# Macaron block on Trainium2: transposes one group later, a first head in two parts, paired updates, an early bias

## The chip, the cores and the metric

The kernel runs on one core of one Trainium2 chip. Five engines work side by side, each through its own list of instructions: PE (matrix products), DVE and POOL (elementwise work), ACT (activations and copies) and SP (here it only issues transfers, or DMAs). The metric is the time of one execution on the device in microseconds (us). Three runs of the kernel before took 3453.76, 3454.74 and 3462.36 us; their median, 3454.74, is the time to compare with.

## The reference

One transformer block on x of shape 4 x 1024 x 512 in float32: half a feed-forward layer, attention, and half the same feed-forward layer again.

```python
x = x + 0.5 * ffn(layernorm(x))
x = x + attention(layernorm(x))
x = x + 0.5 * ffn(layernorm(x))

def ffn(x):                      # 512 -> 2 x 2048 -> 512
    gate, up = split(x @ quant(w_gate_up).T)
    return rms_norm(silu(gate) * up) @ quant(w_proj).T

def attention(x):                # 32 query heads, 8 key heads, 16 wide
    Q, K = rope(x @ Wq.T + bq), rope(x @ Wk.T + bk)
    V = x @ Wv.T + bv
    w = softmax(Q @ K.T / 4)     # 1024 x 1024 for each head
    return (w @ V) @ Wo.T + bo
```

`quant` rounds each group of 64 weights to -1, 0 or 1 times the group's mean magnitude, in bf16.

## The kernel before

**Tiles and blocks.** x stays on the chip in tiles of 128 rows (`xt[b, i]`, eight for each batch). The feed-forward layer works on blocks of 512 rows (four tiles), so there are eight blocks for the first half layer and eight for the second. It splits the 2048 hidden columns into 16 chunks. To keep precision, an operand is split into a rounded part and a remainder (`xT` and `xL`, `high` and `low`), and both are multiplied.

**The order of work is written by hand.** Inside `tc.manual_schedule()` each engine executes its instructions in the order in which the code issues them, and waits at an instruction until its inputs and the buffer it writes are free. The DMAs that a queue issues (SP's by `nc.sync`, POOL's by `nc.gpsimd`) stand in the same order as that engine's other work. So moving a call in the code moves its instructions on every engine at once.

**The stages.** They follow each other:

- The first stage (to about 217 us in the profile) quantises and transposes the weights, and runs the first half layer of blocks 0 and 1 beside it. `First.group(i)` (L639 to L683) is one round: it finishes earlier chunks, turns the three weight parts of chunk i (`transpose`, L490), starts the products of chunk i (`start`), and lets DVE quantise the next weights (`signs`, `quantize`, `scales`). In rounds 0 and 1 it also normalises two of the four tiles of block 1 each and transposes them: `normalize` yields for each tile a function that transposes it on PE, copies it on ACT (`xT`) and subtracts on DVE (`xL`); these are called `turn`. The rest of block 1's projections follows in `projection`, to about 265 us.
- An input stage for each batch (`input_output`, L810 to L847) makes Q, K and V. Its loop goes over eight tiles, with work of several tiles in flight: `turn_in` transposes tile n, `project` multiplies tile n-1, `rotate` (DVE and POOL) and `turn` (PE transposes `pqT`, then writes of `d_q` and `d_k` to memory by SP) finish tile n-2. At n from 5 to 8 it prepares the four tiles of the next feed-forward block. In batches 1 to 3 it also runs the output product of the batch before: `put(i)` multiplies tile i of the attention's result `aT` with the output weights into `pa`, adds the bias on DVE (`ao`) and adds that to x on POOL. `put` 0 to 5 stand in the loop, 6 and 7 after it. `aT` is a load from memory, multiplied on POOL by the reciprocals `rec` of the softmax's sums (`divide`, L996 to L1016, in three steps: `invert`, `spread`, `multiply`).
- A feed-forward stage (`FeedForward.chunks`, L310 to L345). Products with the projection follow their hidden chunk two chunks behind. When the last chunk of a block is projected, `factors` computes the norm and `end` updates the four tiles of x on DVE, and SP stores them if the block is finished. Beside it runs the first part of the maxima, below (`early`).
- An attention stage (`Attention.run`, L1143 to L1238) of 128 steps: eight groups of four query heads that share a key head, two halves of queries, eight tiles of keys. A step computes scores `s`, exponentials `e` on ACT, and the product `o` with V, one step later. The softmax's row maxima come from a second pass over the scores: `maxima` (L1050) computes `sm` on PE, and DVE reduces it. For each group the maxima are turned to `mrow`, written to memory (`d_m`, a DMA on POOL's queue), read back as `mT`, and subtracted by a third product in the scores. Most steps hold two maxima; some hold four, where the number left demands it: `READY` is the step by which the last ought to be complete.
- After the last attention an output stage without an input (`output`, L792 to L808), then the last feed-forward stage.

**Loads for the heads.** `Places` keeps buffers of three tiles and loads them in a fixed order as they come free. `load_heads` (L728) loads the queries and the keys of a group as three DMAs on SP: `p_m<-d_q`, and `p_m<-d_k` twice, for the maxima; `p_s` has the same for the scores. With `places.slow` set, a load's DMAs are queued as pieces, and `piece` issues one.

```python
READY = (HKV - 1) * STEPS - 4                    # 108
places.done(("in", new.b))                       # after the loop
places.load(("m", new.b, 0))
```

Of the kernel before, what the change touches and what calls it, by code (L numbers as in the profile page):

```python
# [10 lines left out]
F32 = mybir.dt.float32  # L11
# [3 lines left out]
ALU = mybir.AluOpType  # L15
# [4 lines left out]
P = 128  # L20
D = 512
H = 2048
HQ, HKV, HD = 32, 8, 16
# [8 lines left out]
DC = D // P  # L32
# [4 lines left out]
def tile_macaron_block(  # L37
# [17 lines left out]
    nc = tc.nc  # L55
    B, T, _ = x.shape
    NT = T // P
# [28 lines left out]
    xt = {}  # L86
# [54 lines left out]
    class FeedForward:  # L141
# [135 lines left out]
            nc.vector.tensor_scalar(half, inv, 0.5, None, ALU.mult)  # L277
            return half

        def end(self, k, half):  # L280
            b, tb, which = self.blocks[k]
            new = waiting.pop(0) if which == "z" and waiting else None
            if new is not None:
                slots[new] = slots[b, tb]
            for i, t in enumerate(self.tiles(k)):
                nc.vector.scalar_tensor_tensor(  # L286
                    t, self.pos[k][i], half[:, i : i + 1], t, ALU.mult, ALU.add
                )
# [20 lines left out]

        def chunks(self):  # L310
            last = len(self.order) - 1
            due = []
            for n, (k, hc) in enumerate(self.order):
                if self.beside is not None:
                    places.piece()
                parts, rest = self.hidden(k, hc)
                due.append((k, hc, parts))
                behind = due.pop(0) if len(due) > self.LAG else None
                if behind is not None:
                    self.project(*behind, [0, 1])  # L320
                if n == last:
                    rest()
                if self.beside is not None:
                    self.beside(self.ps, (n - self.begin) / (last - 1 - self.begin))
                if behind is not None:
                    self.project(*behind, [2, 3])
                    if behind[1] == HC - 1:
                        self.end(behind[0], self.factors(behind[0]))
                if n < last:
                    rest()  # L330
                if k + 1 < len(self.blocks) and 4 <= hc < 12 and hc % 2 == 0:
                    for turn in self.normalize(k + 1, [hc // 2 - 2], self.wp, self.ps, "gu"):
                        self.later.append((hc + 1, turn))
                for step in [step for step in self.later if step[0] == hc]:
                    self.later.remove(step)
                    step[1]()

            for i in range(4):
                for behind in due:
                    self.project(*behind, [i])  # L340
                if i == 1:
                    half = self.factors(k)
            self.end(k, half)
            for _, step in self.later:
                step()  # L345

    class First(FeedForward):
# [7 lines left out]
        def groups(self):  # L355

            self.kept = tc.tile_pool(name="kept", bufs=1)
            self.banks = tc.tile_pool(name="fp0a", bufs=4, space=PSUM)
            self.keep, self.ps = self.kept.__enter__(), self.banks.__enter__()
            self.w, self.wb, self.wide, self.twice, self.q = {}, {}, {}, {}, {}  # L360
            self.sg, self.made, self.units, self.parts, self.turns = {}, {}, {}, {}, []
# [277 lines left out]
        def group(self, i):  # L639
# [13 lines left out]
            if i < 2:  # L653
                if i > 0:
                    self.start(0, i)
                some = [2 * i, 2 * i + 1]
                self.signs(i + 1)
                self.quantize(i + 1)
                steps = self.scales(i + 2)
                scales = normal_scales(self.tiles(1, some), f"0a_1_{i}")  # L660
                for turn in self.normalize(1, some, self.wp, self.ps, "gu", 4, scales):
                    turn()
            else:
                steps = self.scales(i + 2)
                self.start(1, i - 2)
                self.signs(i + 1)
# [60 lines left out]
    def load_heads(key, tiles):  # L727

        _, b, g = key
        q, k = at[b].d_q, at[b].d_k  # L730
        sources = [q[g * G * HD : (g + 1) * G * HD].rearrange("m r t -> (m r) t")]
        for part in range(2):
            keys = k[part, g * HD : (g + 1) * HD].rearrange("d r t -> (d r) t")
            sources.append(keys.unsqueeze(0).to_broadcast([G, 2 * HD, T]))
        return [
            lambda t=t, src=src: nc.sync.dma_start(t.bitcast(F32), src)
            for t, src in zip(tiles, sources)
        ]

# [68 lines left out]
        turns[3]()  # L808

    def input_output(new, old, put, then, wp, ps):  # L810
        turn = None
        for n in range(NT + 2):
            if n == 0:
                new.normalize(0, wp, new.scales(0))
            if 1 <= n <= NT:
                new.project(n - 1, ps)
            if n >= 2:
                new.rotate(n - 2)
            scales = new.scales(n + 1) if n + 1 < NT else None
            after = normal_scales(then.tiles(0, [n - 5]), f"f_{new.b}_{n}") if 5 <= n < 9 else None  # L820
            if n >= 2:
                new.rotated_sum(n - 2)
            if scales is not None:
                new.normalize(n + 1, wp, scales)
            behind, turn = turn, None
            if after is not None:
                (turn,) = then.normalize(0, [n - 5], wp, ps, "pt", 2, after)
            if behind is not None:
                behind()
            if put is not None:  # L830
                for i in {4: (0,), 5: (1,), 6: (2,), 7: (3,), 8: (4,), 9: (5,)}.get(n, ()):
                    put(i, range(DC))
            if n < NT:
                new.turn_in(n, wp, ps)
            if n >= 2:
                new.turn(n - 2, wp, ps)
            if put is not None and n == 1:
                old.after.pop(0)()
                old.after.pop(0)()
            if put is not None and n == 2:  # L840
                old.after.pop(0)()

        places.done(("in", new.b))
        places.load(("m", new.b, 0))
        if put is not None:
            for i in (6, 7):
                put(i, range(DC))  # L847

    class Attention:

# [15 lines left out]
        STEPS = NB * NT  # L866
        ITEMS = NT * 2
        TOTAL = HKV * ITEMS * G
        READY = (HKV - 1) * STEPS - 4
        FIRST = 3  # L870
        EARLY = (3 * ITEMS - 1) * G

# [43 lines left out]
                    [xt[self.b, i]], f"a_{self.b}_{i}", wp, "xa", 2, scales  # L916
                )

        def turn_in(self, i, wp, ps):
            label = f"a_{self.b}_{i}"  # L920
            self.xTs[i] = wp.tile([P, DC, P], F32, tag="axT", name=f"axT_{label}", bufs=2)
            turned(self.rows.pop(i), label, ps, "pt", self.xTs[i])

        def project(self, i, ps):
            pq = ps.tile([P, D], F32, tag="pq", name=f"pq_{self.b}_{i}", bufs=2)
# [65 lines left out]
        def divide(self, c, wp):  # L991
# [12 lines left out]
            def invert():  # L1004
                nc.vector.reciprocal(narrow, narrow)
                nc.sync.dma_start(d_r.rearrange("h (a t) -> h a t", t=n), narrow)
                nc.sync.dma_start(a, self.d_o[at, 0])

            def spread():
                nc.sync.dma_start(rec, d_r.unsqueeze(1).to_broadcast([8, HD, T]))  # L1010
# [7 lines left out]
        def project_out(self, wp, ps, bufs):  # L1018
# [4 lines left out]
            pas = {}  # L1023

            def put(i, chunks):
                if i == 0 and DC - 1 in chunks:
                    nc.sync.dma_start(b_o, bo.partition_broadcast(P))
                if 0 in chunks:
                    pas[i] = ps.tile([P, D], F32, tag="pa", name=f"pa_{b}_{i}", bufs=bufs)
                for n, w in enumerate(w_out):  # L1030
                    for c in chunks:
# [319 lines left out]
```

## Time and profile before

| what | value |
|---|---|
| median of three runs | 3454.74 us |
| the profiled execution | 3450.52 us |
| its span | 3448.8 us |
| mean granted PE clock | 0.977 |
| PE busy | 3317.4 us, 96% |
| DVE busy | 2172.1 us, 63% |
| ACT busy | 1763.7 us, 51% |
| POOL busy | 936.0 us, 27% |

The profile is of one execution. An engine is busy while one of its instructions runs; the time in which it waits is put down to the instruction that it waited for, by the name of what that one wrote. PE is busy in nearly all of the span, and its idle time is spread over a hundred short waits. The granted clock tells how much of its full rate PE had: the same instruction takes longer at a lower one. A row such as `PE sm L1061 <- DMA p_m<-d_k` reads: PE's instruction that writes `sm` at line 1061 waited for the DMA that writes `p_m` from `d_k`.

The stages in the profile, from the starts of their instructions: input stages at about 265 to 331 us, 990 to 1075, 1735 to 1820 and 2478 to 2560; attention at about 650 to 990, 1403 to 1735, 2147 to 2478 and 2892 to 3216; the output stage from 3216 to 3262; feed-forward between them and to the end.

### The profile page before, as it was taken

How to read it: one execution, taken by the hardware profiler on the slowest of the kernel's cores; microseconds unless marked ns; L12 is line 12 of the kernel's file. 1: busy time of each engine (PE TensorE's matmuls, PEld its weight loads, DVE VectorE, ACT ScalarE, POOL GpSimd, SP SyncE). 2: the span in 40 equal slices, each digit the busy share in tenths (PEclk: the TensorE clock that was granted, in tenths of full speed). 3: DMA queues.
4: the chain of work that ended last, by engine and by line, in shares of the span. 5: the costliest groups of instructions: out<-in, count | busy, mean ns of one | idle time of the engine just before them, and what ended most of it. 6: DMA issues, size and time to landing. Idle time of an engine off the chain costs nothing.

```text
span 3448.8 us, 57082 instructions
## 1 busy us (share of the span) xinstructions
PE 3317.4 (96%) x22744; PEld 2150.2 (62%) x22744; DVE 2172.1 (63%) x3626; ACT 1763.7 (51%) x2346; POOL 936.0 (27%) x907
## 2 busy tenths in 40 slices
PE   4998999999999999999999999999999999999899
PEld 3777777644467777544477777444577776444587
DVE  6976666677635666777355666777256656775243
ACT  4752333577742333688723333788523334788343
POOL 2663433200123343100033333000143332010244
PEclk7999999999999999999999999999999999999999
DMA  3533222122313223133123221222231221232111
GB/s 99 155 115 91 69 76 77 44 89 94 101 59 97 69 72 101 51 104 102 65 76 90 82 76 55 73 93 91 82 108 54 81 89 56 94 98 71 30 46 56
DMA packets 206507, 278.47 MB, mean 81 GB/s; under 512 B 25248, under 2 KB 151200, under 8 KB 206240
## 3 DMA queue, kind: packets, MB, share of 16 engines
q1 hardware_dynamic: 201120, 272.70, 25.6%
q8 instruction: 179, 2.93, 0.4%
q0 software_dynamic: 5120, 2.11, 0.3%
q14 instruction: 88, 0.72, 0.1%
HBM read 216.01 MB, written 58.72 MB: 80 GB/s over the span
## 4 chain that ended last, share of the span: by engine, by line
PE 84%; DVE 6%; DMA 3%; issue 3%; POOL 2%; ACT 1%; SPq 0%; POOLq 0%; DVEq 0%; ACTq 0%
PE gu L211 22%; PE s L1158 18%; PE o L1179 14%; PE po L251 12%; PE sm L1061 7%; PE pq L929 3%; PE pa L1032 2%; PE gu_0a L533 2%; DMA p_m<-d_k 1%; DVE pm L1070 1%; PE pkv L929 1%; DVE x L286 1%; DMA rec<-d_r 1%; PE pxn L136 1%; PE po_0a L251 1%
## 5 line engine op out<-in xcount | busy, mean ns | idle before, releaser
L1070 DVE TENSOR_REDUCE pm<-sm 128x1 f32<-128x512 f32 x2048 | 1284.6, 684 | 385.3 <-PE sm L1061 381.7
L1169 ACT ACTIVATE e<-s 128x1024 f32<-128x1024 f32 x1024 | 996.4, 1022 | 326.3 <-PE s L1158 323.5
L1061 PE MATMUL sm<-p_m,p_m 32*128 32x512 f32 x4096 | 768.7, 440 | 31.4 <-DMA p_m<-d_k 10.3
L211 PE MATMUL gu<-xT,guT 128*128 128x512 f32 x1792 | 707.3, 395 | 0.7 <-ACT xT L137 0.7
L211 PE MATMUL gu<-xL,guT 128*128 128x512 f32 x1792 | 701.7, 392 | 0.3 <-DVE xL L139 0.3
L1158 PE MATMUL s<-p_s,p_s 32*128 32x512 f32 x4096 | 679.0, 441 | 0.2 <-ACT e L1169 0.2
L1158 PEld LDWEIGHTS s<-p_s,p_s 32*128 32x128 f32 x4096 | 315.5, 186 | 457.6 <-ACT e L1169 435.2
L1179 PE MATMUL o<-e,vs 128*32 128x512 f32 x4096 | 557.4, 617 | 1.8 <-ACT e L1169 1.8
L1061 PEld LDWEIGHTS sm<-p_m,p_m 32*128 32x128 f32 x4096 | 356.1, 184 | 125.5 <-DVE h L223 65.7
L1158 PE MATMUL s<-mT,ones_r 2*128 2x512 f32 x2048 | 414.3, 399 | 7.1 <-DMA mT<-d_m 6.9
L231 POOL TENSOR_TENSOR sq<-h 128x512 f32<-128x512 f32 x210 | 218.4, 1040 | 710.2 <-DVE h L223 707.7
L221 ACT ACTIVATE sg<-gu 128x512 f32<-128x512 f32 x224 | 133.8, 597 | 497.2 <-PE gu L211 497.1
L211 PEld LDWEIGHTS gu<-xT,guT 128*128 128x128 f32 x1792 | 339.1, 189 | 75.1 <-ACT xT L137 1.0
L223 DVE TENSOR_TENSOR h<-sg,gu 128x512 f32<-128x512 f32 x224 | 153.8, 687 | 367.1 <-PE gu L211 365.8
L211 PEld LDWEIGHTS gu<-xL,guT 128*128 128x128 f32 x1792 | 338.8, 189 | 70.1 <-DVE xL L139 0.6
L251 PE MATMUL po<-w_pT,high 128*128 128x512 f32 x896 | 373.0, 416 | 0.0
L251 PE MATMUL po<-w_pT,low 128*128 128x512 f32 x896 | 353.0, 394 | 0.1
L237 ACT CAST high<-h 128x512 fp32r<-128x512 f32 x224 | 139.0, 620 | 341.9 <-DVE h L223 337.7
L100 ACT CAST guT<-g 128x512 fp32r<-128x512 bf16 x448 | 274.7, 613 | 12.3 <-ACT guT L100 5.8
L235 POOL TENSOR_TENSOR acc<-acc,sq 128x512 f32<-128x512 f32 x205 | 275.5, 1344 | 16.1
L251 PEld LDWEIGHTS po<-w_pT,high 128*128 128x128 f32 x896 | 169.1, 189 | 97.8 <-issue 66.4
L1099 POOL DMA_DIRECT2D d_m<-mrow x32 | 18.9, 591 | 757.2 <-DVE mrow L1097 757.2
(145 smaller groups left out, 3226.2 us busy)
## 6 DMA issues: line engine op xcount, KB each, us to landing
g<-d_guT SPq DMA_DIRECT2D x448, 128.0 KB
p_m<-d_k SPq DMA_DIRECT2D x64, 512.0 KB
p_s<-d_k SPq DMA_DIRECT2D x64, 512.0 KB
p_m<-d_q SPq DMA_DIRECT2D x32, 512.0 KB
p_s<-d_q SPq DMA_DIRECT2D x32, 512.0 KB
d_o<-oT SPq DMA_DIRECT2D x64, 256.0 KB
x<-in_L_attn_x_dram SPq DMA_DIRECT2D x32, 256.0 KB
w<-in_L_ffn_w_gate_up_dram SPq DMA_DIRECT2D x32, 256.0 KB
```

What stands on the lines that cost most here:

```text
L100: nc.scalar.copy(w, t)
L211: nc.tensor.matmul(pg, lhsT=self.weights[k, hc][part][:, c, :], rhs=xp[:, c, :], start=(c == 0 and low == 0), stop=(c == DC - 1 and low == 1),
L223: nc.vector.tensor_tensor(h, sg, gu[1], ALU.mult)
L231: nc.gpsimd.tensor_tensor(sq, h, h, ALU.mult)
L235: nc.gpsimd.tensor_tensor(acc, acc, sq, ALU.add)
L237: nc.scalar.copy(high, h)
L251: nc.tensor.matmul(self.pos[k][i], lhsT=h[:, i * P : (i + 1) * P], rhs=w_pT[hc], start=(hc == 0 and n == 0), stop=(hc == HC - 1 and n == 1),)
L1061: nc.tensor.matmul(s, lhsT=q[at, i * P : (i + 1) * P], rhs=k[part][at, half * 512 : (half + 1) * 512], start=(part == 0), stop=(part == 1),)
L1070: nc.vector.tensor_reduce(pm[:, i, j, half : half + 1], s, AX.X, ALU.max)
L1158: nc.tensor.matmul(s[:, e, :], lhsT=k[part][at, keys] if part < 2 else ones_r[at, :], rhs=(q if part < 2 else self.mrows[g])[at, queries], ...
L1169: nc.scalar.activation(w, s, AF.Exp, scale=1.0 / HD**0.5)
L1179: nc.tensor.matmul(o[j * SLOT : (j + 1) * SLOT, :], lhsT=vs[:, kc, g, :], rhs=es[j // 2][:, j % 2, :], start=(kc == 0), stop=(kc == NT - 1),)
```

## The change

It has six parts.

- In rounds 0 and 1 of the first stage the transposes of block 1 are kept in `turning`, and called one round later, behind the products of that round.
- In batch 0's input stage the transposes have two PSUM banks in place of one (`banks`).
- The first group's load is six DMAs in place of three: 896 columns, then 128. It begins in the loop's last round (n = 9), ahead of `turn(7)`; the rest follows after the loop. `put(6)` moves into that round too. Since `load_heads` is also used for `p_s`, the first scores are loaded in six DMAs as well.
- `end` updates tiles 0 and 1 of x at once, and 2 and 3 after the next chunk's `hidden`.
- The output bias `b_o` is loaded on POOL's queue and added to x on POOL as `put` begins; when the product is there, DVE adds it to x at once. The load of `aT` also moves from SP's queue to POOL's.
- `READY` is one step less.

```diff
-        def end(self, k, half):
+        def end(self, k, half, some=range(4)):
             b, tb, which = self.blocks[k]
-            new = waiting.pop(0) if which == "z" and waiting else None
-            if new is not None:
-                slots[new] = slots[b, tb]
-            for i, t in enumerate(self.tiles(k)):
+            if 0 in some:
+                new = self.new = waiting.pop(0) if which == "z" and waiting else None
+                if new is not None:
+                    slots[new] = slots[b, tb]
+            new = self.new
+            for i, t in zip(some, self.tiles(k, some)):
...
                 parts, rest = self.hidden(k, hc)
+                if ends:
+                    self.end(*ends.pop(), [2, 3])
...
                     if behind[1] == HC - 1:
-                        self.end(behind[0], self.factors(behind[0]))
+                        half = self.factors(behind[0])
+                        self.end(behind[0], half, [0, 1])
+                        ends.append((behind[0], half))
...
-                for turn in self.normalize(1, some, self.wp, self.ps, "gu", 4, scales):
+                rows = list(self.normalize(1, some, self.wp, self.ps, "gu", 4, scales))
+                for turn in self.turning:
                     turn()
+                self.turning = rows
             else:
+                for turn in self.turning:
+                    turn()
+                self.turning = []
                 steps = self.scales(i + 2)
                 self.start(1, i - 2)
...
+        parts = [slice(0, T)] if g > 0 else [slice(0, T - P), slice(T - P, T)]
         return [
-            lambda t=t, src=src: nc.sync.dma_start(t.bitcast(F32), src)
+            lambda t=t, src=src, at=at: nc.sync.dma_start(t.bitcast(F32)[:, at], src[..., at])
+            for at in parts
             for t, src in zip(tiles, sources)
         ]
...
-        turn = None
+        turn, banks = None, 2 if put is None else 1
...
+            if n > NT:
+
+                places.slow = True
+                places.done(("in", new.b))
+                places.load(("m", new.b, 0))
+                for _ in range(3):
+                    places.piece()
...
-                (turn,) = then.normalize(0, [n - 5], wp, ps, "pt", 2, after)
+                (turn,) = then.normalize(0, [n - 5], wp, ps, "pt", 2, after, banks)
...
-                for i in {4: (0,), 5: (1,), 6: (2,), 7: (3,), 8: (4,), 9: (5,)}.get(n, ()):
+                for i in {4: (0,), 5: (1,), 6: (2,), 7: (3,), 8: (4,), 9: (5, 6)}.get(n, ()):
                     put(i, range(DC))
...
-        places.done(("in", new.b))
-        places.load(("m", new.b, 0))
+        places.rest()
+        places.slow = False
         if put is not None:
-            for i in (6, 7):
-                put(i, range(DC))
+            put(7, range(DC))
...
-        READY = (HKV - 1) * STEPS - 4
+        READY = (HKV - 1) * STEPS - 5
...
-                nc.sync.dma_start(a, self.d_o[at, 0])
+                nc.gpsimd.dma_start(a, self.d_o[at, 0])
...
-                if i == 0 and DC - 1 in chunks:
-                    nc.sync.dma_start(b_o, bo.partition_broadcast(P))
+                if i == 0 and 0 in chunks:
+                    nc.gpsimd.dma_start(b_o, bo.partition_broadcast(P))
                 if 0 in chunks:
+                    nc.gpsimd.tensor_tensor(xt[b, i], xt[b, i], b_o, ALU.add)
...
-                    ao = wp.tile([P, D], F32, tag="ao", name=f"ao_{b}_{i}")
-                    nc.vector.tensor_tensor(ao, pas[i], b_o, ALU.add)
-                    nc.gpsimd.tensor_tensor(xt[b, i], xt[b, i], ao, ALU.add)
+                    nc.vector.tensor_tensor(xt[b, i], pas[i], xt[b, i], ALU.add)
```

More of the change, by code (lines that the diff above doesn't have):

```diff
@@ L311, in chunks @@
             last = len(self.order) - 1
-            due = []
+            due, ends = [], []
             for n, (k, hc) in enumerate(self.order):
@@ L360, in groups @@
             self.w, self.wb, self.wide, self.twice, self.q = {}, {}, {}, {}, {}
-            self.sg, self.made, self.units, self.parts, self.turns = {}, {}, {}, {}, []
+            self.sg, self.made, self.units, self.parts = {}, {}, {}, {}
+            self.turns, self.turning = [], []
             for n in range(4):
@@ L830, in input_output @@
             if put is not None:
-                for i in {4: (0,), 5: (1,), 6: (2,), 7: (3,), 8: (4,), 9: (5,)}.get(n, ()):
+                for i in {4: (0,), 5: (1,), 6: (2,), 7: (3,), 8: (4,), 9: (5, 6)}.get(n, ()):
                     put(i, range(DC))
             if n < NT:
-                new.turn_in(n, wp, ps)
+                new.turn_in(n, wp, ps, banks)
             if n >= 2:
@@ L917, in normalize, with turn_in @@
                 )
-        def turn_in(self, i, wp, ps):
+        def turn_in(self, i, wp, ps, banks):
             label = f"a_{self.b}_{i}"
             self.xTs[i] = wp.tile([P, DC, P], F32, tag="axT", name=f"axT_{label}", bufs=2)
-            turned(self.rows.pop(i), label, ps, "pt", self.xTs[i])
+            turned(self.rows.pop(i), label, ps, "pt", self.xTs[i], bufs=banks)
         def project(self, i, ps):
```

## The prediction

> **What bounds the kernel now.** I read the page first: the span is 3448.8 us (the profiled execution 3450.52), PE is busy for 3317.4 of it, 96%, and holds 84% of the chain that ended last. A change that removes no PE work can therefore give back at most the 131 us in which PE stands, and what its matmuls lose at a lower granted clock. So the second view is the list of what PE waited for:
>
> ```profile
> engine line waited for: us in total, times, longest us
> PE pxn_0a L136 <- DVE xn_0a L125: 34.5, 5, 14.9
> PE pqT L976 <- DVE p_t L967: 12.7, 7, 4.3
> PE sm L1061 <- DMA p_m<-d_k: 10.3, 3, 3.8
> PE sm L1061 <- DVE h L223: 9.6, 9, 1.2
> PE gu_0a L533 <- ACT guT L498: 9.2, 4, 3.8
> ...
> PE s L1158 <- DMA mT<-d_m: 6.9, 3, 3.0
> ...
> PE pa L1032 <- POOL aT L1013: 5.2, 1, 5.2
> PE pxn L136 <- DVE xn L125: 5.0, 2, 4.8
> ```
>
> Each row is a place that the change touches; 83 us stand here. A row counts in full only if nothing else is late at that place just after, so each place was read in its own timeline, beginning with the first stage, where PE's rows show start, duration, shape and the wait ahead:
>
> ```profile
> 42.91 1.11 PE L136 MATMUL pxn_0a<-ident,xn_0a 128*128 128x128 f32 x4 [14.87 <-DVE xn_0a L125]
> ...
> 52.85 0.79 PE L533 MATMUL gu_0a<-xT_0a,guT 128*128 128x512 f32 x1 [3.81 <-ACT guT L498]
> ...
> 64.79 1.09 PE L136 MATMUL pxn_0a<-ident,xn_0a 128*128 128x128 f32 x4 [5.96 <-DVE xn_0a L125]
> ...
> 72.27 0.47 PE L533 MATMUL gu_0a<-xT_0a,guT 128*128 128x512 f32 x1
> ```
>
> Last, busy times in stretches: the ends of the four attention stages (last 32 to 34 of 128 steps each), then the first 64 steps of batches 0 and 1; the columns are length, busy time of five engines, and PE's granted clock:
>
> ```profile
> core 0: us, PE busy (x) PEld busy (x) DVE busy (x) ACT busy (x) POOL busy (x), PEclk, DMA share, GB/s
> 905.10:989.80 84.70, 82.05 (x680) 34.12 (x679) 25.15 (x49) 61.20 (x65) 6.60 (x9) 0.92 0.21 65
> 1649.40:1735.20 85.80, 82.31 (x706) 34.14 (x705) 27.04 (x52) 63.68 (x68) 6.59 (x9) 0.96 0.19 64
> 2393.90:2477.70 83.80, 81.57 (x706) 35.16 (x705) 27.05 (x52) 63.45 (x68) 6.61 (x9) 0.96 0.20 65
> 3139.20:3216.30 77.10, 76.34 (x681) 32.82 (x678) 21.48 (x38) 61.17 (x65) 4.93 (x6) 1.00 0.13 44
> 655.20:825.50 170.30, 165.73 (x1697) 73.28 (x1689) 132.96 (x219) 128.42 (x136) 10.13 (x16) 0.99 0.23 75
> 1403.50:1564.60 161.10, 160.00 (x1622) 73.95 (x1620) 123.17 (x204) 124.27 (x132) 10.10 (x16) 0.97 0.25 80
> ```
>
> The fourth end has the same work as the others, no wait for mT in it and a clock of 1.00: it is 6.7 to 8.7 us shorter.
>
> **1. Transposes of the second block, one group later.** PE now waits 14.87 us for the first normalised row of block 1 before it may take the products of weight chunk 1, whose weights were quantised at 37.8. With the transposes behind those products, PE turns the three weight parts next. What was late: the DVE ran two subtractions xL (44.68, 47.71) ahead of h (48.32), and ACT two copies ahead of the cast that guT (52.21) follows. Behind them, h falls to about 43.9, guT to 44.5, and the products start at about 45.1 instead of 52.85. In the second group the row of 64.79 waits for DVE, which quantises to 59.6 and takes scales to 61.4; DVE's next signs start at 73.69 now, after a copy of 72.19 that PE's products release, and at about 65.0 when nothing there waits for the transposes. The gain is what reaches that DVE step, 73.69-65.0 = 8.7; at least the 3.81 that falls away before 52.85 whatever comes later, at most every wait of PE between 37.8, where those weights are ready, and 52.85: 5.1 (42.91-37.8), 1.95, 0.55 and 3.81, or 11.4. I take 8.7, the row that DVE's order sets. Cover: DVE's own quantising; without it the 34.5 comes back elsewhere.
>
> **2. Two banks for the transposes of the first input stage.** There PE waits 1.91, 1.40 and 0.86 for xL at L139, as pxn and pxn_a share a bank, and 4.33 for p_t at 330.07. The p_t chain is started by the last projection, which begins 1.91+1.40 = 3.3 earlier with two banks; the last wait stays. Gain 3.3, bounds 0 and 4.3.
>
> **3. First head in two parts; two output products ahead of the last turn.** In batches 1 to 3 the last pqT waits 1.80, 1.80 and 1.79 for p_t, then two products pa of 3.5 each follow. One of them moves ahead of the turn, longer than the wait: gain 5.4. The DMAs p_m<-d_q and p_m<-d_k were issued at 1073.2 to 1074.9 (batch 1), behind the writes of the last tile, landed 17.04 later, and sm waited 3.66, 2.79 and 3.83 (10.3); the matmuls after it are slow (sm 0.69 against 0.44) and lose, summed over the stretch to the next full-speed row, 1.3, 0 and 2: 3.3 more. Now seven eighths of the columns are issued at about 1067.5, ahead of tile 7's writes, and need seven tiles only; they land near 1083.5, PE wants them at about 1085.5. The last 128 columns follow the writes and land near 1088.5; the second group of maxima needs them at about 1092. Three more issues on SP cost 0.4 to 0.6 each, and wait for part one's landing; behind them on SP is only the fetch of weights three chunks ahead. Gain 13.6; bounds 3 (part one as late as now less the 3 us that its issue moves) and 13.6.
>
> **4. Two DMAs and the add of the bias to POOL.** aT<-d_o goes from SP's queue to POOL's, free of some 3 us of SP issues ahead of it; rec<-d_r behind it on SP goes earlier. In batches 1 and 2 POOL's multiply (2.35) waited 4.68 for rec at 1005.29, ahead of the rotation, and PE stood 0.73 and 2.04: gain 2.8. Against it, b_o's load is now issued on POOL at the first output product and x+=b_o (1.27) waits for it, with the rotation of the next tile queued behind: the load lands 4 to 6 us after issue (d_m's small load: 1.8 to 8.0, median 4.2), the rotation follows some 5 to 6 later. I charge 1, from 0 to 6 (2 per batch).
> The Trainium skill, page "DMA: Bandwidth & Descriptors", section "Issuing engines are not separate DMA queues", says that DMAs of all engines end on the same 16 DMA engines, and that another issuer saves only the issue time. By it the 2.8 would be 0 to 1 and the sum 2 us less; the trace has the aT load waiting on SP's order, not on bandwidth (DMA 0.2 busy), so I keep 2.8.
>
> **5. Updates of x in pairs.** At eight block ends in the four long feed-forward stages, sm waits 0.84 to 1.25 for h (9.2 in all), because DVE runs four updates x (2.73 together) ahead of h. With two updates ahead, h comes 1.37 earlier, more than any wait; the last two follow h and only delay the next po, whose first product is one chunk away (about 11 us). Gain 9.1, bounds 4 and 9.6. The four waits for x (3.3) are at stage ends and stay.
>
> **6. The last output stage.** Now each x of a tile passes ao on DVE (0.69), then POOL (1.26), one buffer between: 2.07 per tile. With b_o added ahead, DVE alone needs 0.69 plus statistics. x0 to x3 are ready at about 3243.9 instead of 3247.5, statistics end at 3247.1, the first transposes run at 3249.2 (now 3253.18, after a wait of 4.76), and the first product at about 3255.9 instead of 3262.46, since products pa no longer stand between: gain 6.5. The multiply that PE awaits for 5.16 is now behind b_o's landing and six adds (6 x 1.27 = 7.6) on POOL, and so is the issue of the last aT load: about 3228 instead of 3223.4. The loads of aT and rec ended together at 3234.8, 11.4 after the first issue; rec now goes first and alone, so the pair ends between 1 earlier and 3 later; I charge 1. Net 5.5, bounds 0 and 8.
>
> **7. Maxima complete one step earlier.** mT arrives one step (2.47) earlier; the waits were 1.97, 3.04, 1.86. Gone with them is the slow stretch: from step 96 to the end the stages take 83.60, 84.69, 82.73 against 75.97: 7.6+8.7+6.8 = 23.1; batch 1 keeps a rest of 0.6. The price: three more steps with four maxima per batch. The first 64 steps of batch 0 hold 16 such, those of batches 1 to 3 hold 4: (170.3-161.6)/12 = 0.72 each, by 12 is 8.7. Net 13.8 (13.5 taken); bounds -9 (waits stay) and 14.
> A rule speaks against the larger term: the page "TensorE: Matmul & The Clock Gate", section "The two states you'll see", gives about 3.4 us of idleness before the clock falls. By it waits of 2 to 3 us cost only themselves, 6.9-8.7 = -1.8, and the whole sum would be 15 less. The rows differ: o's eight matmuls take 1.94 after the 1.97 wait and 1.07 before it.
>
> **Sum.** 8.7 + 3.3 + (5.4+13.6) + (2.8-1) + 9.1 + 5.5 + 13.5 = 60.9. On the profiled execution 3450.5-60.9 = 3389.6; the median of the runs is 4.2 above it: about 3394.
>
> **Rivals.** (a) mT stays late, since d_m's write and its reading back share DMA engines with tables and loads (d_m to mT 3.7 to 8.2 us): term 7 becomes -8.7, the time 3416. For it: batch 1 had 8.2. Against: one step is longer than two of the three waits. (b) The split load lands no earlier, as d_k's loads use few engines and tile 7's writes go between: 13.6 less, 3408. For it: 17 us for 512 KB. Against: six us earlier issue. (c) Slower: PE fills so far that the granted clock falls; mean 0.977 over 3317 us of PE work, so below 0.977 x (1-60.9/3317) = 0.959 everything is eaten, 0.955 gives about 3470. For it: first 64 steps of batch 1 with 99% busy PE show 0.97, of batch 0 with 97% 0.99. Against: the fullest end of all (99%) has 1.00. (d) The edit in the first stage gives only 3.8: 3399.
>
> **How the numbers follow.** Forecast (with (d) and small misses) 0.68, (a) 0.12, (b) 0.14, (c) 0.04, other 0.02. Forecast's own 3384 to 3402; with both (a) and (b) 3416 and above. Range 3382 to 3418. A measurement here tells 0.3%, about 10 us, from no change. Faster 0.93, same 0.03, slower 0.04.
>
> **What would show it.** Right: no sm<-p_m, mT or 14.87 row among PE's waits; ends of attention near 76 us; first gu of the last feed-forward stage at 6 to 7 after its own shift. Wrong: a new wait behind POOL's b_o (rotation, p_t), for SP's second part, or a granted clock under 0.96.

## The result, and the profile after

The changed kernel took 3424.97 us (median of 3423.36 to 3435.27, four runs), the kernel before 3455.78 beside it (3453.76 to 3462.36): a ratio of 0.9914, with a 95% interval of 0.989 to 0.9938, or about 30 us. Half of the 61 us that were predicted came. The two profiled executions lie 24.5 us apart (spans 3448.8 and 3424.3); what follows splits 24.0 of those, up to the last instructions behind the products.

Cut at the first product of each stage, and at the exponentials of steps 0, 96 and 120 of each attention stage, the two traces give these lengths (us):

| stretch | before | after | gained |
|---|---|---|---|
| first stage | 265.5 | 254.0 | 11.5 |
| input stage, batch 0 | 65.6 | 60.2 | 5.4 |
| input stages, batches 1 to 3 | 253.0 | 251.1 | 1.9 |
| feed-forward stages 0 to 3 | 1302.9 | 1304.1 | -1.2 |
| attention, steps 0 to 95, four batches | 987.6 | 997.3 | -9.7 |
| attention, steps 96 to 119, four batches | 256.6 | 245.3 | 11.3 |
| attention, steps 120 to the end | 83.0 | 83.0 | 0.0 |
| output stage | 48.3 | 42.3 | 6.0 |
| last feed-forward stage | 182.4 | 183.5 | -1.1 |

The first stage and batch 0's input stage gave more than they were to give (8.7 and 3.3), the output stage about as much (5.5). The input stages of batches 1 to 3 were to give 7.2 (5.4 from the product moved ahead, 1.8 from the DMAs on POOL's queue) and gave 1.9. The feed-forward stages were to give 22.7 (13.6 from the split load, 9.1 from the pairs) and gave nothing; attention was to give 13.5 and gave 1.6. The list of what PE waits for, in the changed kernel, says why (as before: us in total, times, longest):

```profile
engine line waited for: us in total, times, longest us
PE gu L211 <- ACT guT L100: 12.5, 4, 5.1
...
PE pqT L995 <- DVE p_t L986: 11.1, 4, 5.4
PE pxn_0a L136 <- DVE xn_0a L125: 11.0, 1, 11.0
PE pw L497 <- DVE wq L490: 11.0, 2, 10.4
...
PE sm L1079 <- DVE mrow L1115: 6.1, 6, 1.0
...
PE pa L1052 <- POOL aT L1032: 3.5, 1, 3.5
...
PE s L1176 <- DMA mT<-d_m: 2.8, 3, 1.9
```

The rows aimed at are gone: no sm waits for p_m, and pxn_0a fell from 34.5 to the 11.0 of the kernel's very start (10.4 came back as a wait for wq, the quantising of the next weights: the cover that the prediction named). But three rows are new, or are as long as before. PE now waits 12.5 us for weights, once at the start of each of the four feed-forward stages (5.1, 3.1, 1.1, 3.2); it waits six times for mrow in place of h; and pqT has kept 11.1 of 12.7.

**The wait for weights.** The row at the start of batch 1's feed-forward stage, with what ACT and SP do there, from the three engines' timelines (start, duration, and in brackets the idle time ahead and its releaser):

```profile
1071.03 0.50 PE L211 MATMUL gu<-xT,guT 128*128 128x512 f32 x1 [3.06 <-ACT guT L100]
```

```profile
1064.37 0.61 ACT L100 CAST guT<-g 128x512 fp32r<-128x512 bf16 x1
1069.84 0.62 ACT L237 CAST high<-h 128x512 fp32r<-128x512 f32 x1 [4.86 <-DMA d_k<-qh]
1070.36 0.61 ACT L100 CAST guT<-g 128x512 fp32r<-128x512 bf16 x1
```

```profile
1054.85 1.19 SPq L749 DMA_DIRECT2D p_m<-d_k  x2
1057.52 0.37 SPq L1003 DMA_DIRECT2D d_q<-qh  x1
1057.94 3.12 SPq L1008 DMA_DIRECT2D d_k<-qh  x2
1061.11 0.95 SPq L1003 DMA_DIRECT2D d_q<-ql  x1
1062.10 3.88 SPq L1008 DMA_DIRECT2D d_k<-ql  x2
1070.53 0.32 SPq L749 DMA_DIRECT2D p_m<-d_q  x1
```

Read it from the end. PE's weights guT are late because ACT, which casts them, stood 4.86 us in front of another cast, `high`. That one has its input; it waits for a DMA, the write of tile 7's qh to d_k, since the buffer of `high` lies where the input stage's qh lay. The write is late because the first part of the split load was issued just ahead of it: SP needs 3.12 and 3.88 us to issue two pairs of writes that took 0.94 and 0.99 in the kernel before, where nothing of the load stood ahead of them:

```profile
1069.58 0.94 SPq L989 DMA_DIRECT2D d_k<-qh  x2
1071.11 0.99 SPq L989 DMA_DIRECT2D d_k<-ql  x2
```

That the load ahead is the cause, and the buffer the way, is tested below (u1 and m3).

**The wait for mrow.** DVE and PE at the first block end in that stage:

```profile
1181.61 0.68 DVE L223 TENSOR_TENSOR h<-sg,gu 128x512 f32<-128x512 f32 x1
1182.21 1.40 DVE L288 SCALAR_TENSOR_TENSOR x<-po,half,x 128x512 f32<-128x512 f32 x2
1183.53 0.27 DVE L1115 CAST mrow<-pmT 64x128 fp32r<-64x128 f32 x1
```

```profile
1183.85 0.73 PE L1079 MATMUL sm<-p_m,p_m 32*128 32x512 f32 x5 [1.02 <-DVE mrow L1115]
```

h is now ahead of the second pair of updates, but the copy mrow is behind it, and until that is done a PSUM bank is not free for sm. A wait of 1.24 became one of 1.02. In the kernel before, the row at this place was:

```profile
1200.69 0.92 PE L1061 MATMUL sm<-p_m,p_m 32*128 32x512 f32 x6 [1.24 <-DVE h L223]
```

**The ends of attention.** Steps 96 to 119 of the four batches in the kernel before, then in the changed one (length, busy time and number of instructions of each engine, then PE's granted clock, the share of DMA time, GB/s):

```profile
902.21:969.54 67.33, 65.05 (x553) 27.27 (x547) 25.83 (x48) 48.17 (x51) 6.06 (x8) 0.90 0.25 77
1649.00:1714.96 65.96, 62.80 (x554) 26.24 (x549) 25.84 (x48) 48.19 (x51) 6.06 (x8) 0.95 0.24 79
2393.49:2457.47 63.98, 62.12 (x553) 27.21 (x549) 25.83 (x48) 47.97 (x51) 6.07 (x8) 0.95 0.25 81
3136.36:3195.69 59.33, 59.33 (x551) 26.29 (x547) 23.69 (x41) 47.96 (x51) 4.93 (x6) 1.00 0.16 52
```

```profile
894.30:955.20 60.90, 60.33 (x547) 26.86 (x543) 23.92 (x45) 47.92 (x51) 6.76 (x9) 1.00 0.26 85
1636.66:1697.14 60.48, 60.16 (x547) 26.88 (x543) 23.94 (x45) 47.98 (x52) 6.77 (x9) 1.00 0.25 86
2369.61:2433.93 64.32, 62.42 (x545) 27.56 (x541) 23.92 (x45) 48.14 (x51) 6.75 (x9) 0.95 0.25 81
3117.36:3176.98 59.62, 59.62 (x549) 26.69 (x543) 21.79 (x38) 47.88 (x51) 5.61 (x7) 1.00 0.17 52
```

Batches 0 and 1 lose all but 0.5 us of their wait, and with it the low clock. Batch 2 keeps both: on POOL the write d_m waits for nothing that the trace names until 3.2 us after its input mrow (which ended at 2398.8), and mT comes late again (PE waits 1.90 for it). The first row is d_m at the same place of batch 1, where it starts 0.3 us after its input, the other two are batch 2's:

```profile
1666.34 0.57 POOL L1117 DMA_DIRECT2D d_m<-mrow  x1 [24.04 <-DVE mrow L1115]
2402.04 0.57 POOL L1117 DMA_DIRECT2D d_m<-mrow  x1 [26.80 <-issue]
2408.87 2.06 POOL L1130 DMA_DIRECT2D mT<-d_m  x4 [6.26 <-DMA d_m<-mrow]
```

### The profile page after: what moved, and what is told of

It reads as the page before. It is cut to its first block, busy times and chain, and to the rows that moved or that the text cites. A ratio compares the mean times of both kernels' runs of the same rounds, so it can differ in the third digit from the quotient of the medians.

```text
span 3424.3 us, 57120 instructions
## 1 busy us (share of the span) xinstructions
PE 3312.7 (97%) x22744; PEld 2147.2 (63%) x22744; DVE 2181.3 (64%) x3626; ACT 1765.4 (52%) x2346; POOL 950.3 (28%) x927
## 5 line engine op out<-in xcount | busy, mean ns | idle before, releaser
L1079 PE MATMUL sm<-p_m,p_m 32*128 32x512 f32 x4096 | 769.2, 440 | 22.0 <-DVE pm L1088 11.4
L211 PE MATMUL gu<-xT,guT 128*128 128x512 f32 x1792 | 710.3, 396 | 13.3 <-ACT guT L100 12.5
L237 ACT CAST high<-h 128x512 fp32r<-128x512 f32 x224 | 139.0, 620 | 342.1 <-DVE h L223 320.9
L1176 PEld LDWEIGHTS s<-mT,ones_r 2*128 2x128 f32 x2048 | 198.5, 186 | 31.6 <-DMA mT<-d_m 4.5
```

Source lines behind the costliest of these rows:

```text
L211: nc.tensor.matmul(pg, lhsT=self.weights[k, hc][part][:, c, :], rhs=xp[:, c, :], start=(c == 0 and low == 0), stop=(c == DC - 1 and low == 1),
L237: nc.scalar.copy(high, h)
L1079: nc.tensor.matmul(s, lhsT=q[at, i * P : (i + 1) * P], rhs=k[part][at, half * 512 : (half + 1) * 512], start=(part == 0), stop=(part == 1),)
L1176: nc.tensor.matmul(s[:, e, :], lhsT=k[part][at, keys] if part < 2 else ones_r[at, :], rhs=(q if part < 2 else self.mrows[g])[at, queries], ...
```

## The experiments

Each is the changed kernel with one edit, unless it says otherwise. Ratios are to runs of the kernel before on the same chip (its medians there were 3449.8 to 3452.8 us); the changed kernel's is 0.9914. Of the edits to the changed kernel, only u1 and best1 have intervals that lie clear of its own (0.989 to 0.9938); where another is read against it, the rows of waits and the lengths of stages carry the reading, and the difference of times only agrees with it.

**The first load whole again (u1).** `parts` has one slice, and the load is issued behind the loop:

```diff
-        parts = [slice(0, T)] if g > 0 else [slice(0, T - P), slice(T - P, T)]
+        parts = [slice(0, T)]
...
-                places.load(("m", new.b, 0))
-                for _ in range(3):
-                    places.piece()
...
+        places.done(("in", new.b))
+        places.load(("m", new.b, 0))
```

> The changed kernel with the first head's load whole again and behind the loop, everything else kept. Theory: the first part's reads hold up the writes of tile 7, whose buffer qh lies where the next stage's 'high' is cast, and PE waits for the weights behind that cast (5.1, 3.1, 1.1 and 3.2 us at the starts of the four feed-forward stages, 12.5 in all). Then these four waits vanish here and the waits of sm for p_m come back (about 10 us, with 3 us of slow products behind them): within 5 us of the changed kernel, to either side. Rival: the split load was worth its 13.6 us, and the four waits for weights have another cause (the fetches behind the second part on SP, the output products moved ahead): then this is 10 to 14 us slower than the changed kernel, with both kinds of wait.

Measured: 3436.95 us, 0.9958 (0.9939 to 0.9976), some 15 us slower than the changed kernel. The waits for weights vanish (feed-forward stage 0 gets 6.7 shorter, 317.8), but sm waits 18.1 us for p_m, more than the 10.3 of the kernel before, and stages 1 to 3 are 333 to 334. That the load ahead of the writes makes the weights late stands; the size was wrong, and lies nearer the rival's: with put(6) in the loop, the feed-forward stage begins sooner after the load, so a whole load is later against it. What the third part is worth as a whole takes both undone.

**The third part undone entirely (u5).** As u1, and put(6) behind the loop.

> The changed kernel with the whole third part undone: first load whole and behind the loop, put(6) behind the loop too, as before the change. With the whole load, but put(6) still in the loop, feed-forward stages 1 to 3 were 3 to 11 us longer than the changed kernel's, since the load then starts later against them. Theory: against this the split saves three waits for p_m (about 3.4 each with 1 to 2 us of slow products behind) and pqT's three of 1.8, and costs four waits for weights (12.5): the feed-forward stages 1 to 3 come out within 3 us of the changed kernel's each, the first one 5 to 7 us shorter, the input stages 1 to 3 1.8 longer each; in all within 6 us of the changed kernel. Rival: the split is worth 10 us or more as a whole; then the stages 1 to 3 are 5 us longer each here.

Measured: 3430.84 us, 0.9947 (0.9927 to 0.9968). Feed-forward stages 1 to 3 take 324.3, 325.9 and 327.8, together 1.7 shorter than in the changed kernel, stage 0 is 6.2 shorter; the three input stages are 11.0 longer, as their waits of pqT (19.7 in all) are back. In the traces the whole part is worth 3.1 us, in the medians' ratios some 11, with intervals that overlap. So split load and put(6) together gave the feed-forward stages nothing; what the third part gave lies in the input stages, where put(6) stands ahead of the last turn.

**'low' takes its buffers ahead of 'high' (m3).** One allocation is moved:

```diff
+            low = wp.tile([P, 512], F32R, tag="low", name=f"low_{label}", bufs=self.LAG + 1)
             high = wp.tile([P, 512], F32R, tag="high", name=f"high_{label}", bufs=self.LAG + 1)
             nc.scalar.copy(high, h)
-            low = wp.tile([P, 512], F32R, tag="low", name=f"low_{label}", bufs=self.LAG + 1)
```

> The changed kernel with one line moved: 'low' takes its buffers ahead of 'high', so that 'high' of the first chunks no longer lies where qh and ql of tile 7 lay. Theory: PE's waits for the weights at the starts of the feed-forward stages (5.1, 3.1, 1.1, 3.2) come from the cast of 'high', which waits for the writes of qh to memory: they fall under 1 us each, or move to DVE's 'low' in part; stages 0 to 3 together 6 to 13 us shorter. Rival: the weights are late because their fetches stand on SP behind the second part: the waits stay as they are.

Measured: 3411.07 us, 0.9891 (0.9848 to 0.9933). The row of PE waiting for weights is gone from the list (12.5 before the edit; PE waits 1.3 for 'low' once), and the four stages take 319.2, 323.0, 323.0 and 326.0 in place of 324.5, 327.4, 322.4 and 329.9: 12.9 less in all. The buffer was the cause, not the fetches of the rival: they stand where they stood.

**The first head's keys by four DMAs for each tensor (m1).** Whole load behind the loop, one DMA for each head's 32 rows:

```diff
+                for j in range(G):
+                    nc.sync.dma_start(t[j * SLOT : (j + 1) * SLOT, at], src[..., at])
```

> The first head's load whole and behind the loop, but its keys loaded by four DMAs for each tensor, one for each head's 32 partitions, instead of one with a broadcast over the heads. Theory: the broadcast load is slow (17 us for two times 512 KB) because its packets run on few of the 16 DMA engines; 32 rows spread over all of them, and the load lands within 6 to 9 us of its issue: no wait of sm for p_m, none for weights, 8 DMAs more to issue (4 us of SP's time). Feed-forward stages 0 to 3 at 317 to 323 us each, 8 to 15 us shorter together than in the changed kernel. Rival: the load is bound by bytes or by the other traffic: it lands 15 us or more after its issue, and the waits for p_m are those of the whole load (9 us of idle PE in each of the stages 1 to 3).

Measured: 3401.73 us, 0.9867 (0.9826 to 0.9907). No wait for p_m and none for weights; the four stages take 317.3, 321.0, 322.8 and 322.5, together 20.5 shorter than in the changed kernel.

**The same in the kernel before, alone (s1).**

> The kernel before with the first head's keys alone loaded by four DMAs for each tensor, in the old place. Theory: the slow broadcast was the only cause of the waits for p_m, so they vanish with nothing in their place: feed-forward stages 1 to 3 from 328, 326 and 330 to 321 to 325 each, 9 to 14 us in all. Rival: eight more DMAs on SP hold up the weights behind them, and a wait for those takes the place: under 5 us.

Measured: 3430.21 us, 0.9933 (0.9905 to 0.996): by its median this edit alone gives 23 us, three quarters of what the whole change gives. No wait for p_m is left. Stages 1 to 3 take 324.6, 321.9 and 322.1, together 15.3 us less than in the kernel before, where 9 to 14 were expected; the other 6 us between the two profiles are spread over stages that the edit doesn't touch. The DMA view shows the reason: the busy share of the 16 DMA engines, in tenths over 40 slices, from 1070 to 1095 us, in the kernel before and then here (the loads are issued from 1073 on in both):

```profile
DMA  9979706786232225522539799877222222236322
```

```profile
DMA  8979804799899994691347894336312345222732
```

The stretches of 2 in the first are loads of keys with the broadcast: from 1087.5 to 1093 the mean share is 0.30. With four DMAs it is 0.95 from 1074.5 to 1079, right behind the issue.

**Updates together again (u2).** `end` does all four tiles at once.

> The changed kernel with all four updates of x together again. Theory: the pairs only trade the wait for h (1.24) against a wait for mrow (1.02), since the copy mrow frees the bank that sm needs and now stands behind the second pair on DVE: six of eight waits give 0.2 each, the two of batch 0 0.85 each, so this is 3 us slower than the changed kernel, with eight waits of 0.85 to 1.25 for h. Rival: the pairs were worth 9 us and the waits for mrow come from elsewhere: 9 us slower, with waits for both.

Measured: 3424.51 us, 0.9918 (0.9891 to 0.9946): no difference to the changed kernel that the intervals tell. The feed-forward stages 0 to 3 are 3.3 us longer in the trace, with sm's wait for h back at 9.8 and no row for mrow.

**The turn of maxima ahead of the second pair (m2).**

```diff
                 if ends:
+                    if self.beside is not None:
+                        self.beside.__self__.turn_rows()
                     self.end(*ends.pop(), [2, 3])
...
+        def turn_rows(self):
+            if self.turning:
+                self.turning.pop(0)()
```

> The changed kernel with the turn of finished maxima (pmT, mrow) issued ahead of the second pair of updates. Theory: mrow behind these updates is what sm waits for (1.02 at six block ends): the waits go, and what is left is under 0.5; the feed-forward stages 1 to 3 have 2 us less idle PE each, 6 us in all (and some slow products less). Rival: another wait of the same size (for the bank of pm, for h) takes the place: idle time as before.

Measured: 3415.33 us, 0.9897 (0.9865 to 0.9928). The row for mrow is gone, that for h has 1.6 in place of 0.5; stages 1 to 3 take 322.3, 321.0 and 320.9, 15.4 shorter than in the changed kernel. Of these, 8.0 is idle time and 7.4 faster products: the granted clock is 1.00 there in all three stages, against 0.98 to 1.00. The wait was as expected; the effect is larger. Of the 8.0, 3.2 are shorter waits for weights, which the edit doesn't touch, and how much of the clock's part belongs to it, one profile doesn't tell. Elsewhere this profile lost: the end of batch 1's attention took 67.97 in place of 60.48, with one wait for mT of 1.2 and a clock of 0.85.

**The load of aT on SP's queue again (u3).**

```diff
-                nc.gpsimd.dma_start(a, self.d_o[at, 0])
+                nc.sync.dma_start(a, self.d_o[at, 0])
```

> The changed kernel with the load of aT on SP's queue again, between the write of the reciprocals and the load of rec. Theory: on POOL's queue that load starts 2.4 us before the write d_r, and holds it up on the shared DMA engines, so rec is issued 3.8 us after the write in place of 1.6, and POOL's multiply comes 1.2 us later after the start of the stage (15.4 against 14.2): here the waits of pqT at the third tile return to about 0.7, 2.0 and 0 (5.7 now), 3 us faster in those stages; the output stage gets the old 5.2 us wait for aT in place of 3.5. In all 1 to 3 us faster. Rival: the later multiply comes from the order on POOL, not from the transfers: no change here.

Measured: 3415.41 us, 0.9898 (0.9869 to 0.9928). pqT waits 8.3 in place of 11.1 (1.0, 1.6 and 0.3 at the third tiles) and the input stages 1 to 3 are 2.7 shorter. Not expected: the wait of pa for aT falls to 2.5, the output stage is 38.1 in place of 42.3, at a clock of 1.00 in place of 0.92, and the slow end of batch 2 is gone with every wait for mT:

```profile
2371.93:2431.71 59.78, 59.78 (x545) 27.05 (x541) 23.95 (x45) 48.06 (x52) 6.06 (x8) 1.00 0.27 87
```

This is the row to hold against batch 2's 64.32 above. That the move of aT's load to POOL's queue brings the 3.2 us is well supported: they stand at this place of batch 2 in all eight profiles that have the load there (the changed kernel, u1, u2, u4, u5, m1, m2, m3), and in none of the five that have it on SP's (the kernel before, t1, s1, u3, best1). How it brings them stays open. The transfer itself can't be it: its last packet ended at 2379.7, 19 us before mrow was ready, and in batches 0, 1 and 3, with the same load ahead, d_m starts within 0.4 us.

**READY as before (u4).** -4 in place of -5.

> The changed kernel with the last maximum at the old step. Theory: the steps with four maxima cost about 10 us in the first 96 steps (three stages 3.5 each), and the waits for mT with the slow steps behind them return some 11 us in steps 104 to 120: within 3 us of the changed kernel, the first 96 steps of each attention stage 2 to 3.5 us shorter, steps 104 to 120 some 4 to 7 longer in the first three batches. Rival: the slow steps behind the waits are the clock's own (they fall wherever they fall), and steps 104 to 120 stay near 40 us: then this is about 10 us faster.

Measured: 3427.06 us, 0.9938 (0.9918 to 0.9959). The first 96 steps are 3.7, 0.1, 0.8 and 1.9 shorter; steps 96 to 119 are 66.0, 60.6, 66.6 and 59.3 in place of 60.9, 60.5, 64.3 and 59.6. In the trace's sum that is 0.6 us slower; the ratio lies 8 us to the slower side, with intervals that overlap. The rival (10 us faster) falls. Of the price, 3.9 us are a row of idle time, sm waiting for pm: 7.5 in the kernel before, 11.4 in the changed kernel, 7.1 here. Batch 1's end stays short even with the old step; the theory had three long ends.

**The first part alone, on the kernel before (t1).**

> The kernel before with the first part of the change alone (transposes of block 1 one group later). Theory: the first stage is a matter of DVE's order, and this part gives what the changed kernel's first stage shows: 254 us to the first projection in place of 265.5, nothing elsewhere: 10 to 12 us faster than the kernel before. Rival: part of the 11.5 is the clock's (0.93 granted there in place of 0.90) and comes by chance: 6 to 9 us.

Measured: 3441.76 us, 0.9968 (0.9948 to 0.9987), or 11 us. The first stage takes 255.0. The rival, that a part is the clock's, falls: in s1 the old code of this stage ran at the same 0.93 and took 266.1.

**All mended (best1).** m1, m2 and u3 together.

> The changed kernel with its three new waits mended: keys of the first head by four DMAs for each tensor, whole and behind the loop; the turn of maxima ahead of the second pair of updates; the load of aT on SP's queue. Theory: the gains add up, as they are of different places: 10 to 13 us from the first, 4 to 6 from the second, 5 to 10 from the third: a ratio of about 0.983 to 0.986 to the kernel before, 3392 to 3400 us. Rival: idle time and slow clock are bound together, and what is gained in one place is lost in slow stretches elsewhere: above 0.987.

Measured: 3390.6 us, 0.9821 (0.9793 to 0.985), 62 us faster than the kernel before and the fastest of all kernels here. The feed-forward stages take 317.6, 319.9, 319.0 and 320.0 with 5 us of idle PE in all, and the ends of attention 60.1, 60.1, 60.1 and 59.6. The gains add up: the three differences from 0.9914 would give 0.9834, which lies in the interval. That the prediction, too, had 61 us for the change is chance: 16 us (m1) to 23 us (s1) of the 62 come from the load's shape, which it didn't touch.

## Why the prediction was half right

Direction and mechanisms of the first-stage, bank and output terms were right; the sum was twice too large. The steps that failed: in term 3 the delay of the writes behind the split load was put at nothing (12.5 us of waits for weights came in its place), in term 5 the next instruction on DVE was (6.1 for mrow), term 7's slow stretches were put at 23.1 where 19.3 were there and 11.3 went, and the larger half of term 4 had the wrong sign.

1. **Transposes one group later**: 8.7 predicted, 11.5 in the profile, 11 alone. The mechanism came as forecast: the first product was to start at 45.1 and DVE's step at 65.0; they start at 46.40 and 65.77, in a profile in which PE's first instruction comes 1.2 later (10.99 for 9.75). The row that DVE's order sets was the right one to take, if a little low.
2. **Two banks**: 3.3 predicted, 5.4 in the profile. The last wait (330.07) grew from 4.33 to 5.41, the three others went. The 5.4 holds some of the clock's: at a clock of 0.94 the stage takes 65.6 before and 62.0 to 62.1 after (u2, u3, u5), at 0.97 to 0.98 it takes 63.9 before (t1, s1) and 60.2 after. At like clocks the gain is 3.5 to 3.7, so the term was right.
3. **Split load**: 19.0 predicted (5.4 and 13.6). The 5.4 came: the last pqT of batches 1 to 3 doesn't wait any more. The 13.6 did not, and this is the step that failed. The first part was to be issued "ahead of tile 7's writes", and their delay was put at nothing; "behind them on SP is only the fetch of weights three chunks ahead" looked at SP's queue behind the second part and not at the memory: the writes behind the first part release qh, and `high` lies on qh. In place of 10.3 us of waiting for p_m came 12.5 of waiting for weights. u5 puts the whole part at 3.1 us in the traces (11.0 in the input stages, -7.9 in the feed-forward stages), m3 names the buffer, and m1 shows that the 13.6 were there to be had. Rival (b), "the split load lands no earlier", had the right place and price but not the mechanism: the load did land in time.
4. **DMAs on POOL's queue**: 2.8-1 predicted, and the sign was wrong for the larger half. pqT's wait at the third tile of batches 1 to 3 went from 0.7, 2.0 and 0.2 to 2.0, 1.7 and 2.0. In batch 1 aT's transfer is issued 2.4 us ahead of d_r's write, and the load of rec is issued 3.8 us behind that write, not 1.6; u3 gives 2.7 back in these stages. The rule that I set against the row, that all queues end on the same DMA engines and another issuer saves only the issue time (the Trainium skill, "DMA: Bandwidth & Descriptors", "Issuing engines are not separate DMA queues"), fits this better than my reading, which put the value of the move at 2.8. The charge for b_o's load, 1, wasn't due: POOL waited 3.16 for it in batch 1, and the next rotation stood ready behind it in time.
5. **Pairs**: 9.1 predicted; by u2 3.3 in feed-forward stages 0 to 3, less 1.1 in the last one (182.4 in u2 as before the change, 183.5 with the pairs), and nothing that the times can tell. "With two updates ahead, h comes 1.37 earlier, more than any wait" was right, and sm then waits for the next thing on DVE: mrow, 1.02 at six of eight places. m2 removes it.
6. **Output stage**: 5.5 predicted, 6.0 measured. Profiles of the same code have 40.8 to 43.9 for this stage (38.1 and 39.7 with aT's load on SP's queue), of the old code 46.4 to 48.3: the size is right, to some 2 us.
7. **Maxima one step earlier**: 13.5 predicted, 1.6 measured. The price was well sized: 8.7 predicted, 9.7 in the trace, 6.5 by u4. The gain, 23.1, was mis-sized twice. The ends were cut unevenly: the windows of batches 1 and 2 hold 706 PE instructions and those of batches 0 and 3 some 680, about one step more, which I took for slowness ("The fourth end has the same work as the others" was not so). Cut at steps 96 and 120, the excess over batch 3 is 8.0, 6.6 and 4.7, or 19.3. Then batch 2 kept its wait, which came with term 4's move of aT's load. With that out of the way (u3), the four ends sum to 239.1, 17.5 less than before.

The clock rule that I set against term 7, about 3.4 us of idleness before the clock falls (the Trainium skill, "TensorE: Matmul & The Clock Gate", "The two states you'll see"), doesn't fit these rows: batch 2's wait of 1.90 leaves 62.42 us of busy PE at 0.95 where 59.8 do without a wait. The wait of 1.02 for mrow at 1183.85 was enough: the changed kernel's granted clock is 1.00 from 1176 to 1184, 0.50 from 1185.3 to 1188.6 and 1.00 again from 1189 on. Rival (c), a falling clock, did not come: 0.983 after, 0.988 in the fastest kernel.

## What to carry to other kernels

When an early transfer is to hide a wait, follow its victims as well: what is queued behind it on the DMA engines, whose buffer that releases, and who is allocated on the same bytes. When an update is moved behind the instruction that is waited for, look at what stands behind the update; removing one wait of 1.2 us uncovered one of 1.0. And before a load is split or moved, look at how much of the DMA engines' time it fills: the load's shape was the fault here, and mending it was worth more than moving it: 15.3 us in the stages concerned (s1), against a loss of 7.9 there (u5).

## What the runs showed of the hardware

- Loads of 128 partitions whose source is broadcast over four heads ran at a mean share of 0.30 of the DMA engines' time (1087.5 to 1093 us, kernel before); as four DMAs of 32 rows each, the share was 0.95 (1074.5 to 1079, s1). The price is six more issues on SP for the two tensors of keys: 5.89 us in s1 and 4.14 in m1, in place of 1.20.
- An idle PE of 1 to 3 us was followed by a lower granted clock in many places, not in all. Of the four attention ends in the kernel before, those with a wait (1.9 to 3.0) have 0.90 to 0.95, the one without 1.00; behind a wait of 1.02 the clock was 0.50 for some 3 us (above); in m2, behind a wait of 1.2 at 1665.5, it was 0.50 from 1667 to 1686. But behind the wait of 3.06 for weights at 1071.0 in the changed kernel it stayed at 1.00. What decides, no run here shows. The fastest kernel, with the least idle time, also has the highest mean clock, 0.988 against 0.977.
- A write on POOL's queue (d_m) started 3.2 us after its input was ready, with no releaser in the trace, at one place of all eight profiles that have a 512 KB load on that queue, though in the changed kernel the load had ended 19 us before; it started at once in the five without.
- The clock moves a stage by several us from one profile to the next: the 1603 recorded products of a feed-forward stage took 318.4 to 323.8 us in the changed kernel's three. A difference under 5 us in one stage of one profile therefore counts as an effect only where a row of waits goes with it.
